# Factorization kernel, prologue and epilogue: linear-layer sums in another pool, one set of x sums on GpSimd, the last squares added on VectorE

## The chip, the cores and the metric

The kernel runs on one core of a Trainium2 chip. The metric is device time in microseconds (us), the median of several runs. The kernel before takes 1424.27 us (three runs, 1423.39 to 1424.46). All times inside the kernel are from one profiled execution of 1423.96 us, whose span of recorded work is 1422.2 us; a time such as "at 44.5" counts from the start of that span.

## What is computed

```python
def _L0_rec_ref(x, weight, lin_w, lin_b):      # x 1024x512, weight 64x512x512, float32
    out_lin = x @ lin_w.T + lin_b
    xv = jnp.einsum('bf,efm->bem', x, weight)
    zp = jnp.einsum('bf,efm->bem', jnp.square(x), jnp.square(weight))
    interaction = 0.5 * jnp.sum(jnp.square(xv) - zp, axis=1)
    return out_lin + interaction
```

The second product is linear in the squared weights, so the squares are summed over the 64 embeddings first and multiplied once, at the end. What remains is 64 products of a 1024x512 by a 512x512 matrix, each squared and summed.

## The kernel before

**Tiling.** Two embeddings are treated together (32 pairs, index `q`). Each pair is a 2x2 block problem that is solved with seven products in place of eight (Strassen's scheme in Winograd's form), and each of the seven is split once more in the same way. There are thus 7 outer products per pair, called "1" to "7" and run in the order 1, 2, 6, 5, 7, 3, 4, and 7 inner products in each. A product needs sums of blocks of x as the stationary operand (`xs`, for every outer and inner index, made once), sums of blocks of the weights as the moving operand (`to` for the outer sums, `ti` for the inner ones, made for each pair), and sums of results (`z`).

**Engines.** TensorE multiplies in float32; an inner product is two matmuls of 256 columns, each recorded as two. GpSimd makes `to` (line 321) and `ti` (lines 332, 339, 340) and issues the DMAs that add the squares to `acc[0]`, `acc[1]` (line 455) and the squared weights to `w2_sum` (line 475). VectorE makes the x sums (`outer_x`, lines 143 to 150; `inner_x`, 157 to 160; `a21_sums`, 224 to 227) before the loop, and adds TensorE's results from PSUM in it (lines 405, 407, 421). ScalarE copies PSUM banks and squares. SyncE loads weights and stores the result.

**Order.** Nothing is scheduled by a tool: `st.at(t, fn)` puts a piece of work at a time of a written-out schedule, and the list sorted by `t` is the order in which every engine receives its instructions, which it works off strictly one after the other. One unit of `t` in the loop is one inner product on TensorE. Pair q begins at 49 q; times below zero are the prologue. A pool hands out its buffers in turn, and who asks for one that is still being read waits for the reader: `zpool` (tag "z") has 6, `tipool` (tag "ti") 3, `topool` 3.

**The prologue.** TensorE first runs matmuls on constants (`spin`, lines 179 and 181), then `x @ lin_w.T`: the first half of the rows in 16 plain matmuls (`lin`, line 195), the second half (`lin_p`, line 241) with seven inner products for each half of the contraction. `lin_p("5")`, `("6")` and so on multiply by sums of lin_w in the two buffers `LT`, made by GpSimd at t = -30, with x sums from `A21_SUMS` (first half) and from `inner_x("4")` (second half). The two `LT` buffers come from `tipool`, as do the first pair's `ti` for products 1, 2, 6, 5. VectorE makes the x sums for outer products 1, 2, the A21 sums, 4, 5, then (after a `lin_join`, line 261, that waits for TensorE) 6, again a `lin_join`, then 7 and 3; after them comes its first work of the loop, `join("y", "s5", 3)` of product 1 (line 421, t = 8.5), which TensorE's seventh inner product of product 1 (t = 12) waits for, since both use PSUM bank y.

**The epilogue.** After the last pair (g = 49 x 32 = 1568) the product of squared x and summed squared weights is made for two groups of rows, s = 0 and s = 1, seven inner products of 8 recorded matmuls each (line 589). VectorE halves `acc` and adds the bias (`last_t`, line 618, two instructions for each s and r), adds that to blocks of the output (`add_t`, line 648), and combines PSUM banks (`minus_half`, line 635). Eight stores follow (line 643). `acc[1]` is complete only when the squares of the last `c21` have been added to it, at t = g + 9.65, by a DMA that GpSimd issues (line 455).

Of the kernel before, what the change touches and what calls it, by code (L numbers as in the profile page):

```python
# [8 lines left out]
F32 = mybir.dt.float32  # L9
# [19 lines left out]
def kernel(  # L29
# [30 lines left out]
    nc = tc.nc  # L60
    _, _, _, Q = x.shape
    E, F, M = weight.shape
    P = 128
    NK = F // P
    HM = M // 2
    BK = 2 * HM
# [4 lines left out]
    tipool = ctx.enter_context(tc.tile_pool(name="tipool", bufs=3))  # L71
    w2pool = ctx.enter_context(tc.tile_pool(name="w2pool", bufs=2))
    spool = ctx.enter_context(tc.tile_pool(name="spool", bufs=3))
    zpool = ctx.enter_context(tc.tile_pool(name="zpool", bufs=6))
# [8 lines left out]
    acc = [  # L83
        const.tile([P, 4, BK], F32, tag=f"acc{r}", name=f"acc{r}") for r in range(2)
    ]

    def xsl(i, o):
        return xs[:, SLOT[i], SLOT[o], :]

    st = Stream()  # L90
# [31 lines left out]
    def quarter(r, kk, n):  # L122

        w = slice(0, 3) if n is None else n
        for i, rk in BLOCK.items():
            if rk == (r, kk):
                return a21[i] if n == 3 else xs[:, SLOT[i], w, :]
        return A21[:, w, :]

    def outer_x(i):  # L130
        if i in BLOCK:
            return []

        def put(n):
            w = slice(0, 3) if n is None else n

            def of(o):
                return a21[o] if n == 3 else xs[:, SLOT[o], w, :]

            def src(r, kk):  # L140
                return quarter(r, kk, n)

            if i == "5":
                nc.vector.tensor_add(of(i), src(1, 0), src(1, 1))
            elif i == "6":
                nc.vector.tensor_sub(of(i), of("5"), src(0, 0))
            elif i == "7":
                nc.vector.tensor_sub(of(i), src(0, 0), src(1, 0))  # L148
            else:
                nc.vector.tensor_sub(of(i), src(0, 1), of("6"))  # L150

        return [lambda: put(None), lambda: put(3)]

    def inner_x(i):
        add, sub = nc.vector.tensor_add, nc.vector.tensor_sub
        return [
            lambda: add(xsl(i, "5"), a21[i], xsl(i, "4")),  # L157
            lambda: sub(xsl(i, "6"), xsl(i, "5"), xsl(i, "1")),
            lambda: sub(xsl(i, "7"), xsl(i, "1"), a21[i]),  # L159
            lambda: sub(xsl(i, "3"), xsl(i, "2"), xsl(i, "6")),  # L160
        ]
# [3 lines left out]


    A21_SUMS = zpool.tile([P, 4, Q], F32, tag="z", name="A21_sums")
    LT = [tipool.tile([P, 4, HM], F32, tag="ti", name=f"lt{kk}") for kk in range(2)]
    LIN = {}

    def spin():

        one = nc.const_aps.tensor(1.0, [P, BK], mybir.dt.bfloat16)
        zero = nc.const_aps.tensor(0.0, [P, BK], F32)
        for n in range(3):
            ps = psum.tile([P, BK], F32, tag="y", name=f"y_spin{n}", bufs=3)
            nc.tensor.matmul(ps, one[:, 0:P], one, start=True, stop=True)
        for _ in range(2):  # L180
            nc.tensor.matmul(ps, zero[:, 0:P], zero, start=True, stop=True)

    def lin(kk):

        order = [(s, j, l) for s in range(2) for j in range(2) for l in range(2)]
        if kk == 0:
            order.sort(key=lambda o: o[2])
        for s, j, l in order:
            n = 2 * s + j
            if kk == 0 and l == 0:  # L190
                tag = "xxvv"[n]
                LIN[n] = psum.tile(
                    [P, M], F32, tag=tag, name=f"lin{n}", bufs=2 if tag == "x" else 3
                )
            nc.tensor.matmul(  # L195
                LIN[n],
                quarter(0, kk, (0, 1, 3, 2)[2 * s + l])[:, ts(j, P)],
                lw_sb[:, 2 * kk + l, :],
                start=(kk == 0 and l == 0),
                stop=(kk == 1 and l == 1),  # L200
            )
# [10 lines left out]
    def lin_x(kk, o):  # L212
        if kk == 1:
            return xsl("4", o)
        return A21[:, SLOT[o]] if o in "124" else A21_SUMS[:, "5673".index(o)]
# [14 lines left out]
    def lin_p(o, bank, first):  # L230
        def fn():
# [7 lines left out]
            for kk in range(2):  # L239
                for j in range(2):  # L240
                    nc.tensor.matmul(  # L241
                        LIN[bank][:, ts(j, HM)],
                        lin_x(kk, o)[:, ts(j, P)],
                        operand_b(lw_sb[:, ts(kk, 2)], LT[kk], o),
                        start=(first and kk == 0 and j == 0),
# [13 lines left out]
    def lin_join(bank, s, blk):  # L259
# [5 lines left out]
        return fn  # L265

    st.at(-40, spin)
    for kk in range(2):
        st.at(-30 + 8 * kk, lambda kk=kk: lin(kk))
        st.at(-30 + kk, lambda kk=kk: sums_t(LT[kk], lw_sb[:, ts(kk, 2)]))  # L270
    for n in range(4):
# [70 lines left out]
    def inner_t(q, i):  # L342
        TI[q, i] = tipool.tile([P, 4, HM], F32, tag="ti", name=f"ti{q}_{i}")
        sums_t(TI[q, i], outer_b(q, i))

    def operand_b(b, t, o):
        return {
            "1": lambda: b[:, 0, 0:HM],
            "2": lambda: b[:, 1, 0:HM],
            "3": lambda: b[:, 1, HM:M],  # L350
            "5": lambda: t[:, 0, :],
            "7": lambda: t[:, 1, :],
            "6": lambda: t[:, 2, :],
            "4": lambda: t[:, 3, :],
        }[o]()
# [14 lines left out]
    Z = {}  # L370
# [74 lines left out]
    def squares(t, q, name, r, wait=5):  # L445
        def sq():
            z = Z[q, name]
            for h in range(2):
                o = z[:, ts(h, 2)]
                nc.scalar.activation(o, o, AF.Square)  # L450

        st.at(t, sq)
        st.at(
            t + wait,
            lambda: nc.gpsimd.dma_start(acc[r], Z[q, name], accum_op=ALU.add),  # L455
        )
# [32 lines left out]
    for q in range(NQ):  # L489
        g0 = 49 * q  # L490
        st.at(-100 if q == 0 else g0 - 48.8, lambda q=q: load_w(q))
        for n, i in enumerate(ORDER):
            t0 = g0 + 7 * n
            lead = t0 - 7.5
            if i == "6":
                st.at(lead - 8, lambda q=q: outer_t(q, "5"))
                st.at(lead - 4, lambda q=q: outer_t(q, "6"))
            if i == "7":
                st.at(lead - 4, lambda q=q: outer_t(q, "7"))
            if i == "4":  # L500
                st.at(lead - 1, lambda q=q: outer_t(q, "4"))
            st.at(lead, lambda q=q, i=i: inner_t(q, i))
            block_product(t0, q, i, SUMS[i])
            if i == "2":
                squares(t0 + 14.6, q, "c11", 0)
            if i == "7":
                squares(t0 + 14.6, q, "z5", 1)
            if i == "3":
                squares(t0 + 14.6, q, "c12", 0, 5 if q < NQ - 1 else 4)
            if i == "4":  # L510
                if q < NQ - 1:
                    squares(t0 + 14.6, q, "c21", 1)
                else:
                    squares(t0 + 12.65, q, "c21", 1, 1)
        for v in range(2):
            w_squares(g0 + 14.6 + 14 * v, q, v)


    for sums, t in (
        (inner_x("1"), -29),  # L520
        (inner_x("2"), -22),
        (a21_sums(), -20),
        (inner_x("4"), -18),
        *((outer_x(m) + inner_x(m), t) for m, t in zip("5673", (-16, -5, -3, -1))),
    ):
        for n, fn in enumerate(sums):
            st.at(t + 0.1 * n, fn)

    g = 49 * NQ
    h = g - 49
# [76 lines left out]
    def blk(n, s, b):  # L610
        return L[n, s][:, b // 2, b % 2]
# [4 lines left out]
    def last_t(s, r):  # L616
        for u in range(2):
            nc.vector.scalar_tensor_tensor(
                L["t", s][:, r, u].rearrange("p (j c) -> p j c", j=2),
                acc[r][:, 2 * s + u].rearrange("p (j c) -> p j c", j=2),  # L620
                0.5,
                bias[:, ts(u, HM)].unsqueeze(1).broadcast_to([P, 2, HM]),
                ALU.mult,
                ALU.add,
            )
# [15 lines left out]
    def store(s, b):  # L641
        r, u = b // 2, b % 2
        nc.sync.dma_start(
            out_dst[r, s, :, u], blk("o", s, b).rearrange("p (j c) -> p j c", j=2)
        )

    def add_t(s, b):
        nc.vector.tensor_add(blk("o", s, b), blk("o", s, b), blk("t", s, b))
# [8 lines left out]
    for s, ks in ((0, (0, 3.2, 5.2, 6, 7, 8, 9)), (1, (10, 12, 14, 16, 18, 20, 22))):  # L657
# [19 lines left out]
        else:  # L677
            st.at(k2 + 0.5, minus_half("x", s, 0, "t"))
            st.at(k4 + 0.5, minus_half("y", s, 2, "t"))
            for b, k in ((0, k2), (3, k7), (1, k3), (2, k4)):  # L680
                st.at(k + 0.6, lambda b=b: store(1, b))
    for r, t in ((0, 11), (1, 13)):
        st.at(g + t, lambda r=r: last_t(0, r))
        st.at(g + t + 0.1, lambda r=r: last_t(1, r))
        for u in range(2):
            st.at(g + t + 0.2, lambda b=2 * r + u: add_t(0, b))
            st.at(g + t + 0.2, lambda b=2 * r + u: store(0, b))
    for b in (3, 1):
        st.at(g + 15, lambda b=b: add_t(1, b))

    with tc.manual_schedule():
        st.run()
# [30 lines left out]
```

## Time and profile before

| | busy in the profile (span 1422.2 us) | share |
|---|---|---|
| TensorE matmul | 1411.8 us | 99% |
| GpSimd | 1174.4 us | 83% |
| VectorE | 922.2 us | 65% |
| ScalarE | 616.7 us | 43% |

[...]the 99% says who sets the time and not how much is left. The first 50 us and the last 20 us are where the change lies; there the order in time (start, duration, engine, line, operation, operands, count, and in brackets how long the engine had been idle and for whom) says more than the sums. The list of waits names who waited for whom, the total, how often, and the longest. The table by stretches gives the TensorE clock that was granted as a share of the full one.

### The profile page before, as it was taken

What the parts mean: (1) busy time and instruction counts of PE and PEld (TensorE: products, weight loads), DVE (VectorE), ACT (ScalarE), POOL (GpSimd) and SP (SyncE); (2) the same over time, 40 slices, a digit from 0 to 9 for tenths busy, and PEclk for the clock granted to TensorE, in tenths of its full rate; (3) what the DMA queues carried; (4) which work ended last, traced back from release to release, by engine and by line L of the source; (5) the groups of instructions that cost most, each with busy time, mean ns of one, the idle gap of its engine ahead of it and who ended that gap; (6) DMA issues with size and microseconds to landing.
All of it is one profiled execution on the core that took longest, in us unless ns stands there. A gap on an engine that the chain in (4) does not pass through costs nothing.

```text
span 1422.2 us, 18124 instructions
## 1 busy us (share of the span) xinstructions
PE 1411.8 (99%) x6479; PEld 1232.8 (87%) x6479; DVE 922.2 (65%) x1342; ACT 616.7 (43%) x822; POOL 1174.4 (83%) x1041
## 2 busy tenths in 40 slices
PE   9899999999999999999999999999999999999998
PEld 6788888888888888888888888888888888888887
DVE  6756667656667666666665666665666765666665
ACT  2354444454443444444444444445444345444352
POOL 4689888888888888888888888888988888888884
PEclk9999999999999999999999999999999999999999
DMA  5298888899889889889889888889888989998886
GB/s 207 50 212 202 200 197 194 193 204 207 199 197 202 185 194 215 200 200 201 187 189 218 200 200 202 183 198 213 200 200 196 198 189 202 207 203 197 203 175 148
DMA packets 41290, 276.16 MB, mean 194 GB/s; under 512 B 4465, under 2 KB 7025, under 8 KB 8561
## 3 DMA queue, kind: packets, MB, share of 16 engines
q0 software_dynamic: 27504, 200.29, 69.3%
q1 hardware_dynamic: 12976, 72.62, 17.2%
q10 hardware_dynamic: 720, 2.10, 0.4%
q8 instruction: 52, 0.85, 0.2%
q14 instruction: 38, 0.30, 0.1%
HBM read 72.61 MB, written 2.10 MB: 53 GB/s over the span
## 4 chain that ended last, share of the span: by engine, by line
PE 95%; DVE 1%; DMA 1%; POOL 1%; issue 0%; ACT 0%; POOLq 0%; SPq 0%; DVEq 0%
PE y L361 40%; PE x L361 27%; PE v L361 27%; PE lin L195 1%; DMA acc<-z_c 1%; DMA xs<-x 1%; PE y_lin L241 0%; PE x_lin L241 0%; POOL tw L579 0%; DVE a_sb L148 0%; POOL sx L564 0%; POOL z_z L415 0%; DVE xs L159 0%; POOL sx L562 0%; DVE xs L157 0%
## 5 line engine op out<-in xcount | busy, mean ns | idle before, releaser
L361 PE MATMUL y<-ti,xs 128*128 128x256 f32 x2688 | 654.7, 379 | 4.7 <-DVE z_z L421 4.7
L361 PEld LDWEIGHTS y<-ti,xs 128*128 128x128 f32 x2688 | 511.2, 190 | 74.9 <-DVE z_z L421 5.1
L426 ACT COPY y<-x 128x512 f32<-128x512 f32 x224 | 127.7, 570 | 620.8 <-PE x L361 620.8
L361 PE MATMUL x<-to,xs 128*128 128x256 f32 x1024 | 253.1, 380 | 0.0
L361 PE MATMUL v<-ti,xs 128*128 128x256 f32 x896 | 229.9, 379 | 0.0
L361 PEld LDWEIGHTS x<-to,xs 128*128 128x128 f32 x1024 | 195.1, 191 | 26.7
L332 POOL TENSOR_TENSOR ti<-to 128x512 f32<-128x512 f32 x128 | 180.9, 1413 | 33.8 <-PE y L361 30.5
L321 POOL TENSOR_TENSOR to<-w,to 128x1024 f32<-128x1024 f32 x64 | 159.5, 2491 | 45.6 <-PE v L361 45.6
L361 PE MATMUL x<-w,xs 128*128 128x256 f32 x768 | 192.8, 380 | 0.0
L450 ACT ACTIVATE z_c<-z_c 128x1024 f32<-128x1024 f32 x192 | 192.6, 1053 | 0.0
L361 PEld LDWEIGHTS v<-ti,xs 128*128 128x128 f32 x896 | 170.2, 190 | 23.1
L421 DVE TENSOR_TENSOR z_z<-y,s 128x512 f32<-128x512 f32 x128 | 88.0, 687 | 125.6 <-PE y L361 125.6
L361 PEld LDWEIGHTS x<-w,xs 128*128 128x128 f32 x768 | 146.5, 191 | 20.1
L332 POOL TENSOR_TENSOR ti<-w 128x512 f32<-128x512 f32 x96 | 131.0, 1365 | 32.8 <-PE y L361 19.8
L361 PE MATMUL v<-to,xs 128*128 128x256 f32 x512 | 131.4, 379 | 0.0
L455 POOL DMA_DIRECT2D acc<-z_c x96 | 84.1, 876 | 57.1 <-ACT z_c L450 48.4
L405 DVE TENSOR_TENSOR s<-y,z_z 128x512 f32<-128x512 f32 x160 | 110.3, 689 | 28.8 <-PE y L361 22.6
L467 ACT ACTIVATE w<-w 128x1024 f32<-128x1024 f32 x126 | 126.3, 1053 | 0.0
L421 DVE TENSOR_TENSOR z_c<-y,s 128x512 f32<-128x512 f32 x96 | 66.4, 692 | 90.3 <-PE y L361 90.3
L405 DVE TENSOR_TENSOR s<-v,z_z 128x512 f32<-128x512 f32 x160 | 110.1, 688 | 18.4 <-PE v L361 11.4
L421 DVE TENSOR_TENSOR z_z<-v,s 128x512 f32<-128x512 f32 x128 | 87.7, 685 | 38.2 <-PE v L361 38.2
L361 PEld LDWEIGHTS v<-to,xs 128*128 128x128 f32 x512 | 97.3, 190 | 13.2
(112 smaller groups left out, 1617.0 us busy)
## 6 DMA issues: line engine op xcount, KB each, us to landing
acc<-z_c POOLq DMA_DIRECT2D x96, 1024.0 KB, 7.6
w_sum<-w POOLq DMA_DIRECT2D x63, 1024.0 KB, 7.9
w<-weight SPq DMA_DIRECT2D x62, 1024.0 KB, 6.0
acc<-z_z POOLq DMA_DIRECT2D x32, 1024.0 KB, 7.8
xq<-x SPq DMA_DIRECT2D x2, 1024.0 KB, 5.5
out<-o_last SPq DMA_DIRECT2D x8, 256.0 KB, 2.3
w<-weight ACTq DMA_DIRECT2D x2, 512.0 KB, 8.8
w<-weight SPq DMA_DIRECT2D x2, 512.0 KB, 7.8
```

The source lines that it names most:

```text
L195: nc.tensor.matmul(LIN[n], quarter(0, kk, (0, 1, 3, 2)[2 * s + l])[:, ts(j, P)], lw_sb[:, 2 * kk + l, :], start=(kk == 0 and l == 0), stop ...
L321: nc.gpsimd.tensor_sub(t, a, b)
L332: nc.gpsimd.tensor_sub(t[:, 0:2, :], b[:, :, HM:M], b.rearrange("p l m -> p (l m)")[:, 0:M].rearrange("p (u c) -> p u c", u=2),)
L361: nc.tensor.matmul(ps[:, ts(j, HM)], xsl(i, o)[:, ts(j, P)], rhs, start=(start and j == 0), stop=True, skip_group_check=True,)
L405: nc.vector.tensor_add(o, d[bank], Z[q, addend][:, blk])
L421: nc.vector.tensor_add(Z[q, name][:, blk], d[bank], d[s])
L426: st.at(t0 + 0.5, lambda: nc.scalar.copy(d["y"], d["x"]))
L450: nc.scalar.activation(o, o, AF.Square)
L455: lambda: nc.gpsimd.dma_start(acc[r], Z[q, name], accum_op=ALU.add),
L467: nc.scalar.activation(w2[:, ts(h, 2)], W[q, v][:, ts(h, 2)], AF.Square)
```

## The change

It has five parts. The sums of lin_w move from two buffers of `tipool` to one of `zpool`, which is to leave all three `ti` buffers to the loop's first operands. The x sums of outer product 3 (six instructions: 768 columns, 256 columns, and four of 256) move from VectorE to GpSimd, and from t = -1 to t = 14 and after, since they are first read at t = 35. The second constant matmul group of `spin` loses half of one matmul. The squares of the last `c21` are added to `acc[1]` by two VectorE instructions of 1024 columns at t = g + 8.65 in place of the DMA. VectorE's last work is put in another order, so that what row group 1 needs comes before what only row group 0's second half needs.

```diff
-    def outer_x(i):
+    def outer_x(i, eng=nc.vector):
...
-    def inner_x(i):
-        add, sub = nc.vector.tensor_add, nc.vector.tensor_sub
+    def inner_x(i, eng=nc.vector):
+        add, sub = eng.tensor_add, eng.tensor_sub
...
-    LT = [tipool.tile([P, 4, HM], F32, tag="ti", name=f"lt{kk}") for kk in range(2)]
+    lt_sb = zpool.tile([P, 2, 4, HM], F32, tag="z", name="lt_sb")
+    LT = [lt_sb[:, kk] for kk in range(2)]
...
-        for _ in range(2):
-            nc.tensor.matmul(ps, zero[:, 0:P], zero, start=True, stop=True)
+        for n in (HM, BK):
+            nc.tensor.matmul(
+                ps[:, 0:n], zero[:, 0:P], zero[:, 0:n], start=True, stop=True
+            )
...
+        def add(h):
+            z = Z[q, name][:, ts(h, 2)]
+            nc.vector.tensor_add(acc[r][:, ts(h, 2)], acc[r][:, ts(h, 2)], z)
+
         st.at(t, sq)
+        if wait is None:
+            for h in range(2):
+                st.at(t + 3, lambda h=h: add(h))
+            return
...
-                    squares(t0 + 12.65, q, "c21", 1, 1)
+                    squares(t0 + 12.65, q, "c21", 1, None)
...
-        *((outer_x(m) + inner_x(m), t) for m, t in zip("5673", (-16, -5, -3, -1))),
+        *((outer_x(m) + inner_x(m), t) for m, t in zip("567", (-16, -5, -3))),
...
+    for n, fn in enumerate(outer_x("3", nc.gpsimd) + inner_x("3", nc.gpsimd)):
+        st.at(14 + n, fn)
...
-    for r, t in ((0, 11), (1, 13)):
-        st.at(g + t, lambda r=r: last_t(0, r))
-        st.at(g + t + 0.1, lambda r=r: last_t(1, r))
-        for u in range(2):
-            st.at(g + t + 0.2, lambda b=2 * r + u: add_t(0, b))
-            st.at(g + t + 0.2, lambda b=2 * r + u: store(0, b))
-    for b in (3, 1):
-        st.at(g + 15, lambda b=b: add_t(1, b))
+    for t, q, r in ((11, 0, 0), (11.1, 1, 0), (13, 1, 1), (18.7, 0, 1)):
+        st.at(g + t, lambda q=q, r=r: last_t(q, r))
+    for t, b in ((11.2, 0), (11.2, 1), (18.8, 2), (18.8, 3)):
+        st.at(g + t, lambda b=b: add_t(0, b))
+        st.at(g + t, lambda b=b: store(0, b))
+    for t, b in ((13.1, 3), (14.6, 1)):
+        st.at(g + t, lambda b=b: add_t(1, b))
```

More of the change, by code (lines that the diff above doesn't have):

```diff
@@ L143, in put @@
             if i == "5":
-                nc.vector.tensor_add(of(i), src(1, 0), src(1, 1))
+                eng.tensor_add(of(i), src(1, 0), src(1, 1))
             elif i == "6":
-                nc.vector.tensor_sub(of(i), of("5"), src(0, 0))
+                eng.tensor_sub(of(i), of("5"), src(0, 0))
             elif i == "7":
-                nc.vector.tensor_sub(of(i), src(0, 0), src(1, 0))
+                eng.tensor_sub(of(i), src(0, 0), src(1, 0))
             else:
-                nc.vector.tensor_sub(of(i), src(0, 1), of("6"))
+                eng.tensor_sub(of(i), src(0, 1), of("6"))
         return [lambda: put(None), lambda: put(3)]
-    def inner_x(i):
-        add, sub = nc.vector.tensor_add, nc.vector.tensor_sub
+    def inner_x(i, eng=nc.vector):
+        add, sub = eng.tensor_add, eng.tensor_sub
         return [
```

## The prediction, made before the changed kernel ran

> **What bounds the kernel now.** I read the page's shares first (TensorE matmul 99%), then the list of waits for what TensorE still waits on, then the first 50 us and last 20 us in order of time, then the granted clock by stretches. The list of waits has these lines on the change:
>
> ```profile
> POOL ti L332 <- PE y_lin L241: 13.0, 1, 13.0
> PE y L361 <- DVE z_z L421: 4.7, 1, 4.7
> DVE t_last L618 <- DMA acc<-z_c: 2.3, 1, 2.3
> PE y_last L589 <- DVE o_last L635: 0.7, 1, 0.7
> ```
>
> The columns are total us, times, longest. TensorE has two stalls of weight, each once. The first, in order of time:
>
> ```profile
> 43.78 0.68 DVE L421 TENSOR_TENSOR z_z<-y,s 128x512 f32<-128x512 f32 x1
> 44.52 2.07 PE L361 MATMUL y<-ti,xs 128*128 128x256 f32 x4 [4.73 <-DVE z_z L421]
> 46.39 1.91 PE L361 MATMUL x<-w,xs 128*128 128x256 f32 x4
> 48.09 1.78 PE L361 MATMUL x<-to,xs 128*128 128x256 f32 x4
> 49.72 1.03 PE L361 MATMUL y<-ti,xs 128*128 128x256 f32 x4
> ```
>
> The inner product before it started at 38.76 and one takes 0.863 us (start to start, 37.90 to 38.76), so undisturbed the fourth row would start at 38.76 + 4 x 0.863 = 42.2, not 49.72. The gap costs 7.5 us, of which only 4.9 are the wait: the next three products start 1.87, 1.70 and 1.63 us apart. The clock (eighth column) says why:
>
> ```profile
> 42.00:43.00 1.00, 0.00 (x0) 0.00 (x0) 0.93 (x3) 0.00 (x0) 0.00 (x0) 0.90 0.00 0
> 43.00:44.00 1.00, 0.00 (x0) 0.00 (x0) 1.00 (x4) 0.00 (x0) 0.00 (x0) 0.50 0.00 0
> 49.00:50.00 1.00, 1.00 (x5) 0.85 (x4) 0.03 (x1) 0.08 (x1) 1.00 (x2) 0.69 0.00 0
> ```
>
> It halved at 42.8 (0.90) and came back at 49.6 (0.69). VectorE was late because GpSimd held it up. Here is the pattern:
>
> ```profile
> 14.00 0.78 POOL L339 TENSOR_TENSOR ti<-w,ti 128x256 f32<-128x256 f32 x1
> 14.23 0.83 DVE L158 TENSOR_TENSOR xs<-xs 128x256 f32<-128x256 f32 x1
> 15.61 2.53 POOL L321 TENSOR_TENSOR to<-w,w 128x1024 f32<-128x1024 f32 x1
> 15.85 2.56 DVE L160 TENSOR_TENSOR xs<-xs 128x256 f32<-128x256 f32 x1
> 20.25 0.42 DVE L158 TENSOR_TENSOR xs<-xs 128x256 f32<-128x256 f32 x1
> ```
>
> Alone an x sum takes 0.42; beside GpSimd it ends 0.27 us after the GpSimd instruction does (14.78 to 15.06, 18.14 to 18.41), so the two alternate, one each. VectorE's instructions that read PSUM keep 0.68 beside GpSimd. From 18.1 to 31.1 GpSimd waits for an `LT` buffer; its 9 us of work for products 2 and 6 then falls on VectorE's last sums (31 to 40.5).
>
> [...]
>
> **LT in the big pool.** `ti` 2 no longer waits 13 us. `ti` 2, `to` 6 and `ti` 6 (1.45 + 0.78 + 0.79, 2.53, 1.4 + 0.8 + 0.8) run from 18.2 to about 27.2. That relieves 31 to 40, but VectorE's sums between 18.3 and 21.3, until now free, alternate with them. Ends worked out with the 0.27 us: A21 "5" after 18.22 + 1.45, at 19.95; "6" at 20.8; "7" at 21.65; "3" behind `to` 6 (21.4 to 24.0) at 24.3; x4 "5" behind `ti` 6's first (24.05 to 25.5) at 25.75; x4 "6" at 26.6; x4 "7" at 27.45. TensorE needs x4 "5" for the second half of `lin_p("5")`, which before loaded weights at 22.02:
>
> ```profile
> 22.02 0.84 PEld L241 LDWEIGHTS v_lin<-lt,xs 128*128 128x128 f32 x4
> ```
>
> So a new stall of about 25.8 - 22.05 = 3.75 us takes the place of the old wait. "6" is needed 1.7 us after that (27.5) and "7" later, so one stall. Behind it everything shifts by 3.75. GpSimd is then idle until about 44 (it waits for `ti` 1), so VectorE's 6, 7 and two joins run at their free pace: y join at 32.2, 6 done 35.5, v join 36.2, 7 done 39.0; TensorE gives `join("y")` its bank at 36.17 + 3.75 + 1 = 40.9. With product 3's sums gone (2.8 us, 41.00 to 43.78) the old stall is gone whole: -7.5.
>
> Does the new stall halve the clock? TensorE idles about 3.6 us[...]. [...]four runs within 1.1 us suggest that it halved in all of them[...]. I take two in three. [...]
>
> **x sums of product 3 on GpSimd.** No GpSimd instruction of 768 columns is in the trace: between 1.26 (512) and 2.37 (1024), taken 1.8. With five of 256 at 0.8 pitch that is 5.8 us. They queue behind `ti` 5 (done 47.1) and around `to` 7; behind them stands `ti` 7, first part done 56.4. TensorE wants it at product index 27, 31.73 + 3.75 + 27 x 0.863 = 58.8. Margin 2.4 us; `to` 7 has 4, `ti` 3 over 4, and the x sums themselves (55.1) 4 before 59.2. GpSimd's 17% idle absorbs the rest: 0. The later release of `raw_sb` holds `z5` until 49.7, wanted at 56.5: 0.
>
> **Shorter spin.** 0.86 us less of cold matmul, but `lin` then waits for x until 9.27 as now (it already idles 0.33 there): 0.
>
> **The end.** Undisturbed the last product starts at 1413.78 + 1.73 = 1415.5, not 1416.35: 0.85 lost. New VectorE order: two adds of 1024 columns, from pitches 0.34, 0.60 and 0.87 for 256, 512 and 768 about 1.14 each, 1404.2 to 1406.5; four halvings and two adds at 0.6 to 1410.1; two and two to 1412.5; x block; y block 1414.0 to 1414.7, in time for 1415.5. Then two halvings and two adds to 1417.05, v block to 1417.65, last block 1417.65 to 1418.3 where TensorE would allow 1417.5. Against 1419.07: -0.8. The two stores of row group 0 now stand just before the last two; three stores 0.6 apart landed after 2.2, 2.4, 2.5 us, the lone last one after 2.2, so a fourth lands after 2.65: +0.4. Net -0.4.
>
> **Sum, likeliest case.** -7.5 + 3.75 + 1.9 - 0.4 = -2.2, from 1424.0 (the profiled run) to 1424.27 (median): 1421.8 to 1422.0. I take 1421.8.
>
> **Rivals.**
> A, the stall moves but the clock stays full: -4.15, 1420.0. [...] Against: the old stall seems to have halved it every time. 25%.
> B, the forecast, 1420.9 to 1422.9: 45%.
> C, VectorE slips one sum ahead (then 2.2 us of stall and no halving, 1418.4) or GpSimd's early work doesn't hold it up at all (-7.9, 1416.3). Against: at 14.00, 14.86 and 15.61 GpSimd went first each time. 12%.
> D, no gain or slower. The sums on GpSimd take 50% longer (5.8 to 8.7 us), which overruns the margin of `ti` 7 and is passed on to TensorE nearly whole (+2.9), the halving costs its upper bound (3.4 in place of 1.9: +1.5), the stores queue one more time over (+1): 1421.8 + 5.4 = 1427.2; with one of the three alone 1422.8 to 1424.7. Against: margins of 2.4 to 4 us and 17% idle. 18%, of which under half is over 1427.1.
>
> **Numbers.** 0.2% is 2.85 us: 1421.4 and 1427.1. Faster: A 25, C 12, a third of B 15, together 52%; slower 8% (of D); same 40%. Range: 1418.4 to 1424.2 leaves out half of C and most of D.
>
> **What would show it.** Right: TensorE waiting some 3.7 us for an x sum in `lin_p` near 22, GpSimd busy without a break from 12.5 to 27, no wait for VectorE near 40, clock halved at some time between 25 and 33, last product without a wait. Wrong: VectorE's sums of 0.42 us between 18 and 22 beside a busy GpSimd, a wait of TensorE for `ti` 7 near 59, or the last store over 3 us after its block.

## The result and the profile after

The changed kernel takes 1420.59 us (eight runs, 1416.80 to 1422.02) against 1423.94 us before (eight runs, 1423.32 to 1424.46): ratio 0.9973, 95% interval 0.9962 to 0.9984. It is faster by 3.4 us, and its runs are spread over 5 us where those of before lay within 1.1. The profiled run took 1421.11 us, its span 1419.3 us.

The list of waits of the changed kernel (who waited for whom: us in total, times, longest), the lines in which TensorE waits for another engine after the first 10 us. `PEld` is its weight load:

```profile
PEld v_lin L244 <- POOL ti L335: 3.6, 1, 3.6
PE v_lin L244 <- DVE xs L157: 3.2, 1, 3.2
```

Both waits for VectorE that the list of before had, in the loop and at the last product, are gone. One new one, in `lin_p("5")`, stands in their place. (The first line names GpSimd, but its instruction had ended at 24.98, and this product doesn't read `ti`: of the two operands, `lt_sb` was complete at 12.3, and VectorE's sum came at 25.27.) In order of time (start, duration, engine, line, what; in brackets the idle time before):

```profile
17.93 1.44 POOL L335 TENSOR_TENSOR ti<-w 128x512 f32<-128x512 f32 x1
18.17 1.48 DVE L227 TENSOR_TENSOR A_sums<-raw_sb 128x256 f32<-128x256 f32 x1
...
21.07 2.52 POOL L324 TENSOR_TENSOR to<-w,to 128x1024 f32<-128x1024 f32 x1
21.31 2.56 DVE L230 TENSOR_TENSOR A_sums<-raw_sb,A_sums 128x256 f32<-128x256 f32 x1
23.66 1.32 POOL L335 TENSOR_TENSOR ti<-to 128x512 f32<-128x512 f32 x1
23.79 1.48 DVE L157 TENSOR_TENSOR xs<-raw_sb,xs 128x256 f32<-128x256 f32 x1
25.41 1.10 PE L244 MATMUL v_lin<-lt_sb,xs 128*128 128x256 f32 x4 [3.19 <-DVE xs L157]
...
42.25 0.69 DVE L424 TENSOR_TENSOR z_z<-y,s 128x512 f32<-128x512 f32 x1 [1.88 <-PE y L364]
```

GpSimd no longer waits for a buffer and works without a break from 18 to 26.7. VectorE's sums, 0.42 us each in the kernel before at this place, take 0.8 to 2.6 us, one behind each GpSimd instruction; the x4 sum that TensorE waits for ends at 25.3. In the last row the join of product 1 has waited for TensorE (1.88 us), where before TensorE waited for it. The clock of the changed kernel, in the table by stretches (eighth column, as before):

```profile
26.00:27.00 1.00, 1.00 (x6) 0.90 (x5) 1.00 (x3) 0.45 (x1) 0.72 (x1) 0.91 0.00 0
27.00:28.00 1.00, 1.00 (x3) 0.76 (x3) 1.00 (x3) 0.15 (x1) 0.00 (x0) 0.50 0.00 0
30.00:31.00 1.00, 1.00 (x5) 0.83 (x5) 0.13 (x1) 0.21 (x1) 0.00 (x0) 0.88 0.00 0
```

It halved here too, after the new wait, from 26.8 to 30.2: 3.4 us, of which half is lost.

**Where the time went.** Three stretches account for the two profiled runs: from VectorE's first x sum (the moment x has landed and TensorE can go on with `lin`) to the first product of the loop; from there to the 13th product; from the loop's last matmul to the end.

| us | before | after |
|---|---|---|
| x has landed | 9.23 | 9.06 |
| to the loop's first product | 22.50 | 27.61 |
| its first 12 products | 17.98 | 10.49 |
| from the loop's last matmul to the end | 25.9 | 25.6 |

So -7.5 in the loop, +5.1 ahead of it (3.4 of stall and 1.7 of halved clock), -0.3 at the end, -0.2 from the landing of x: -2.9, the difference of the spans.

### The profile page after: what moved, and what is told of

Its sections match the earlier page's. It is cut to its first block, busy times and chain, and to the rows that moved or that the text cites. A ratio compares the mean times of both kernels' runs of the same rounds, so it can differ in the third digit from the quotient of the medians.

```text
span 1419.3 us, 18121 instructions
## 1 busy us (share of the span) xinstructions
PE 1410.8 (99%) x6479; PEld 1232.5 (87%) x6479; DVE 923.2 (65%) x1338; ACT 616.9 (43%) x822; POOL 1179.0 (83%) x1046
## 4 chain that ended last, share of the span: by engine, by line
PE 98%; DVE 1%; DMA 1%; issue 0%; SPq 0%; DVEq 0%
PE y L364 41%; PE x L364 27%; PE v L364 27%; PE y_last L603 1%; DMA xs<-x 1%; PE x_last L603 0%; PE y_lin L244 0%; PE v_last L603 0%; DVE xs L160 0%; DVE xs L157 0%; PE v_lin L244 0%; DVE A_sums L230 0%; DVE xs L158 0%; PE x_lin L244 0%; DVE xs L159 0%; DVE A_sums L227 0%
```

## The experiments

All times are medians beside the kernel before on the same chip, of which there were three (the kernel before took 1423.43, 1423.58 and 1423.82 us on them). Ratios carry 95% intervals. Most runs left no trace, but each has its mean granted clock on record. A stretch of 3.4 us at half clock lowers it by 0.0012, so a run at 1.000 had none. A run at 0.999 may have had one or not, since the clock can also fall once the matmuls are over: in the profiled run of before it was 0.70 from 1421.5 to the end at 1422.2, the last matmul having ended at 1418.3, and the profiled runs of `a_delay` and `a_reorder` have 0.999 without a halved stretch in their first 50 us. No profiled run without such a stretch is below 0.999, so a run at 0.998 is taken to have had at least one.

### The two parts of the prologue, one undone at a time

`a_lt_back` is the changed kernel with the old buffers for the sums of lin_w:

```diff
-    lt_sb = zpool.tile([P, 2, 4, HM], F32, tag="z", name="lt_sb")
-    LT = [lt_sb[:, kk] for kk in range(2)]
+    LT = [tipool.tile([P, 4, HM], F32, tag="ti", name=f"lt{kk}") for kk in range(2)]
```

> The changed kernel with the sums of lin_w back in two tipool buffers, nothing else undone. Theory (moving these sums trades the old stall near 40 for a new one near 22): GpSimd waits again until about 31, no stall near 22; VectorE is free at 41.0 instead of 43.8, so TensorE waits about 2 us near 40[...]: 1423.94 - 7.5 + 2.0 - 0.4 = 1418.0 us, faster than the changed kernel and with less spread than its 5 us. Rival (the gain comes from moving these sums): about 1423.5 us.

Measured 1419.75 us, 0.997 (0.9961 to 0.998), from 1417.88 to 1420.75. The stall near 22 is gone and one of 2 us stands near 40, as expected. In order of time, and below it the clock by stretches:

```profile
41.15 0.68 DVE L423 TENSOR_TENSOR z_z<-y,s 128x512 f32<-128x512 f32 x1
41.88 1.97 PE L363 MATMUL y<-ti,xs 128*128 128x256 f32 x4 [1.94 <-DVE z_z L423]
```

```profile
41.00:42.00 1.00, 0.12 (x1) 0.12 (x2) 0.90 (x3) 0.00 (x0) 0.00 (x0) 1.00 0.00 0
42.00:43.00 1.00, 1.00 (x3) 0.82 (x4) 1.00 (x2) 0.00 (x0) 0.00 (x0) 0.51 0.00 0
```

But the clock halved after it, at 42.0 and for 3.4 us, which the expected 1418.0 has no term for. That costs 1.7 us, as much as the median missed the expectation of 1418.0 by; the three runs with a mean clock of 1.000 took 1417.88, 1417.90 and 1418.94. In this run, then, a wait of 1.94 us went with a halving.

`a_x3_back` is the changed kernel with the sums of product 3 on VectorE again:

```diff
-        *((outer_x(m) + inner_x(m), t) for m, t in zip("567", (-16, -5, -3))),
+        *((outer_x(m) + inner_x(m), t) for m, t in zip("5673", (-16, -5, -3, -1))),
...
-    for n, fn in enumerate(outer_x("3", nc.gpsimd) + inner_x("3", nc.gpsimd)):
-        st.at(14 + n, fn)
```

> The changed kernel with the x sums of product 3 back on VectorE at t = -1. Theory: once GpSimd is idle from 27 to 45, VectorE makes these sums unhindered in 2.8 us before TensorE needs the join, so nothing is lost: 1420.6 us, with the same stall near 22. Rival (these sums leaving VectorE is what removes the old stall): 2.8 us of wait near 42, 1423.4 us.

Measured 1418.56 us, 0.9966 (0.9954 to 0.9979), from 1417.10 to 1421.46: nothing is lost, the rival's 1423.4 is out. That it came out below 1420.6 was not expected, but it lies inside the spread of the changed kernel. Its profiled run (1417.10) shows what a quick run is like:

```profile
8.97 0.42 DVE L157 TENSOR_TENSOR xs<-raw_sb,xs 128x256 f32<-128x256 f32 x1 [8.97 <-DMA xs<-x]
9.43 0.42 DVE L158 TENSOR_TENSOR xs<-xs 128x256 f32<-128x256 f32 x1
9.77 0.42 DVE L159 TENSOR_TENSOR xs<-xs,raw_sb 128x256 f32<-128x256 f32 x1
9.98 1.34 POOL L335 TENSOR_TENSOR lt_sb<-lw_sb 128x512 f32<-128x512 f32 x1 [1.15 <-DMA lw_sb<-lin_wT]
```

The second half of lin_w landed a microsecond after x, so VectorE had begun three sums before GpSimd's second set of lin_w sums began. In the changed kernel's profiled run it had begun one (9.06; GpSimd began at 9.23). Two sums more of a lead are two GpSimd instructions less to wait behind: TensorE's waits ahead of the loop came to 1.2 us in place of 5.1 with the halving.

### Each part alone

`b_lt` is the kernel before with the zpool buffer alone (the first diff reversed); `b_x3` the kernel before with product 3's sums on GpSimd alone.

> The kernel before with nothing changed but the sums of lin_w in a zpool buffer. Theory (this part alone trades the old stall for the one near 22; the x sums of product 3 can stay on VectorE): as the changed kernel but for the end, 1418.5 to 1421 us with its spread of several us. Rival (both parts are needed): 1422 us or more, with a wait of TensorE for VectorE near 42.

> The kernel before with nothing changed but the x sums of product 3 on GpSimd. Theory: the wait near 40 falls from 4.9 to about 2.2 us, the clock still halves after it in most runs[...]: 1423.8 - 2.8 - 0.9 = 1420.1 us, from 1418 to 1421. Rival (the sums on GpSimd hold up ti 7): 1422 or more.

Measured 1418.83 us, 0.9966 (0.9954 to 0.9978), and 1418.84 us, 0.9969 (0.9957 to 0.9981). Either alone gains what both together gain, or more: they are two ways to remove one stall, of which `b_x3` keeps 2 us and `b_lt` nothing, with the new stall in its place. `b_lt` lies within its expectation. `b_x3` is 1.3 us below its own, which had the clock halve in most runs: it did not in the profiled run, and four of six runs have a mean clock of 1.000. Waits of TensorE in `b_lt`, then in `b_x3`:

```profile
PE v_lin L242 <- DVE xs L157: 2.9, 1, 2.9
```

```profile
PE y L361 <- DVE z_z L421: 1.9, 1, 1.9
```

### What the new stall is made of

`a_reorder` is the changed kernel with VectorE's sums in the order in which TensorE wants them:

```diff
-        (inner_x("2"), -22),
+        (inner_x("2"), -17),
...
-        *((outer_x(m) + inner_x(m), t) for m, t in zip("567", (-16, -5, -3))),
+        *((outer_x(m) + inner_x(m), t) for m, t in zip("567", (-5.49, -5, -3))),
```

> The changed kernel with VectorE's first sums in another order: those of x4 right after the A21 sums, those of x2 and x5 (needed only from product 2 and 5 on) after them, x5 behind the first join. The work and GpSimd's queue are the same, so VectorE and GpSimd still alternate. Theory (the stall near 22 is VectorE's x4 sums queued behind 12 others, each held up by one GpSimd instruction): x4 '5' is ready near 21.4, TensorE waits at most 0.5 us near 22 and nowhere else, no halving: 1423.5 - 7.5 + 0.5 - 0.4 = 1416.1 us, with a spread near 1 us. Rival (TensorE would wait for something else there, or the joins behind the moved sums come late): 1418.5 or more.

Measured 1416.02 us, 0.9948 (0.9936 to 0.9959), four of five runs from 1415.68 to 1416.24 and one at 1418.38. It beats both kernels. The alternation is as before, and hurts nobody (in order of time):

```profile
19.54 0.94 DVE L157 TENSOR_TENSOR xs<-raw_sb,xs 128x256 f32<-128x256 f32 x1
...
21.28 2.56 DVE L159 TENSOR_TENSOR xs<-xs,raw_sb 128x256 f32<-128x256 f32 x1
...
22.09 1.03 PE L244 MATMUL v_lin<-lt_sb,xs 128*128 128x256 f32 x4
...
38.00 0.68 DVE L424 TENSOR_TENSOR z_z<-y,s 128x512 f32<-128x512 f32 x1
```

The x4 "5" sum is ready at 20.5, TensorE takes it at 22.09 without a wait, and the first product of the loop starts 22.50 us after x has landed, as in the kernel before. The last row is the join that had started at 43.78 there.

`a_reorder_x3` is this kernel with product 3's sums back on VectorE (the second diff above).

> The kernel with VectorE's first sums reordered, and the x sums of product 3 back on VectorE at t = -1. Theory (with the sums of lin_w in zpool, moving product 3's sums to GpSimd gains nothing): VectorE has them done before it is wanted, or is at most 1 us late: 1416.0 to 1417 us. Rival (moving them is needed, as the kernel before suggests where they were the last 2.8 us): 1418.5 or more.

Measured 1418.34 us, 0.9965 (0.9953 to 0.9978): the rival is nearer. Without the stall near 22, TensorE is early, and VectorE, with 2.8 us more to do, is the later one:

```profile
40.00 0.42 DVE L160 TENSOR_TENSOR xs<-xs 128x256 f32<-128x256 f32 x1
40.34 0.68 DVE L424 TENSOR_TENSOR z_z<-y,s 128x512 f32<-128x512 f32 x1
41.08 1.42 PE L364 MATMUL y<-ti,xs 128*128 128x256 f32 x4 [2.20 <-DVE z_z L424]
```

So the move of these sums is worth nothing in the changed kernel and about 2.3 us in the reordered one (the two were run on different chips, with 0.24 us between their kernels before). The shorter path of TensorE is half of the reason. Counted from the landing of x, the join of product 1 began at 30.7 in the profiled run of `a_x3_back` and TensorE wanted its bank at 31.6; here it began at 32.0 and was wanted at 30.4. That VectorE is 1.3 us later comes with the new order: it waited 3.7 us for a part of x, until 13.6, where in `a_x3_back` it waited 0.4. This is one profiled run of each.

`a_delay` gives GpSimd a useless instruction more, ahead of its second set of lin_w sums:

```diff
     st.at(-40, spin)
+    st.at(-29.5, lambda: nc.gpsimd.memset(acc[0], 0.0))
```

> The changed kernel with one useless GpSimd instruction more: a memset of 2048 columns of acc[0] (overwritten later) between the two halves of the sums of lin_w, so that all of GpSimd's early work starts 1 to 2 us later. Theory (the long stall near 22, and with it the spread, comes from GpSimd's second half of these sums starting within 0.2 us of VectorE's first x sum, so that the two alternate from the start; where it started 1 us later the stall was 0.9): VectorE gets 3 or 4 sums ahead, the stall falls below 1 us, no halving: about 1416.5 us with a spread near 1 us, 4 us faster for 2 us of added work. Rival ([...]GpSimd's work is what TensorE waits for): 1420.6 us or slower, spread as before.

Measured 1417.42 us, 0.9957 (0.9944 to 0.9969), all five runs from 1417.33 to 1417.75. Work added to a busy engine makes the kernel 3 to 4 us faster than the changed kernel and takes its spread away. In order of time:

```profile
8.88 1.81 POOL L271 MEMSET acc<- 128x2048 f32 x1
9.26 0.42 DVE L158 TENSOR_TENSOR xs<-xs 128x256 f32<-128x256 f32 x1
9.60 0.42 DVE L159 TENSOR_TENSOR xs<-xs,raw_sb 128x256 f32<-128x256 f32 x1
9.94 0.42 DVE L160 TENSOR_TENSOR xs<-xs 128x256 f32<-128x256 f32 x1
10.65 1.26 POOL L336 TENSOR_TENSOR lt_sb<-lw_sb 128x512 f32<-128x512 f32 x1
```

This GpSimd instruction, which reads no tensor, did not hold up the three of VectorE's sums that ran whole beside it: at 9.26, 9.60 and 9.94 they took 0.42 us each, where the sums beside GpSimd's own sums took 0.8 to 2.6. What is left against 1416 is a wait of 1.1 us for the first `lin_join`, which stands behind the x5 sums in VectorE's queue; the reordering had moved that too.

### The clock

`a_fill` puts twelve matmuls on constants, whose result is not used, ahead of the waiting product:

```diff
+    SPIN = []
...
+            SPIN.append(ps)
...
             for kk in range(2):
+                if o == "5" and kk == 1:
+                    one = nc.const_aps.tensor(1.0, [P, BK], mybir.dt.bfloat16)
+                    for _ in range(12):
+                        nc.tensor.matmul(
+                            SPIN[2], one[:, 0:P], one, start=True, stop=True
+                        )
```

> The changed kernel with twelve extra bf16 matmuls on constants put in TensorE's queue just ahead of the inner product that waits near 22 (about 2.6 us of work inside the wait; their result is not used). Theory (the changed kernel's time is the stall plus, in most runs, a halved clock after it): the wait ends at the same moment, the clock stays full, 1417 to 1419.4 us, little spread. Rival (the spread has another cause): 1420.6 us and the spread stays.

Measured 1418.59 us, 0.997 (0.9959 to 0.9981). Four of seven runs lie between 1418.29 and 1418.59, the others go up to 1421.05. The profiled one is the slowest. In order of time, and below it the clock by stretches:

```profile
9.84 8.80 PE L200 MATMUL lin<-lw_sb,xs 128*128 128x512 f32 x16 [1.96 <-DMA xs<-x]
...
26.05 0.83 DVE L158 TENSOR_TENSOR xs<-xs 128x256 f32<-128x256 f32 x1
...
27.12 1.02 PE L252 MATMUL v_lin<-lt_sb,xs 128*128 128x256 f32 x4
```

```profile
10.00:11.00 1.00, 1.00 (x3) 0.52 (x3) 0.97 (x2) 0.00 (x0) 1.00 (x1) 0.91 1.03 419
28.00:29.00 1.00, 1.00 (x6) 0.90 (x5) 1.00 (x3) 0.60 (x1) 0.00 (x0) 1.00 0.00 0
```

Nothing halved after the filled wait, but the clock had halved at 10.8, after a wait of 2.0 us for x in `lin`. That made `lin` late, so the filling outlasted the wait: the x4 "5" sum was done at 26.0, and the product behind the twelve matmuls began at 27.12. So the median came out where the theory had it (1417 to 1419.4), and the spread of 2.8 us did not go. In this run the delay comes from the first 10 us; for the others that is not shown.

`a_spin_back` is the changed kernel with the old, longer constant matmuls; `a_again` the changed kernel as it is, to have its spread beside these.

> The changed kernel with the old constant matmuls (0.86 us longer). Theory: lin waits for x until about 9.3 in both, and later for VectorE: 1420.6 us, no difference. Rival (the shorter constant work leaves a gap of up to 2.5 us ahead of 9.5 that halves the clock by itself, as seen in the run with matmuls filled in): about 1 us faster and less spread.

> The changed kernel as it is, to have its spread beside the others on the same chip. All theories: 1420.6 us, from 1416.8 to 1422.

Measured 1420.02 us (0.9973, 0.9963 to 0.9983; 1417.47 to 1421.45) and 1421.20 us (0.998, 0.9972 to 0.9988; 1417.03 to 1423.23). The difference is inside the spread; the runs don't tell whether the shorter spin does anything. (The gap of 2.5 us in the expectation counts from the start of one matmul to the start of the next; the wait in it was 2.0.) It can matter: in the profiled run of `b_x3` (old spin) `lin` was slower at its beginning, its first four matmul records taking 2.40 us from 5.42 to the next ones, where those of `b_lt` (old spin too) took 1.77 from the same moment, as if the clock had come to full only near 6.7 (an estimate from these two, with half the full speed until then); x landed at 8.5, and `lin` reached it at 9.5, a microsecond late. The profiled run of `a_again`, 1423.23 us, is the bad end of the spread: x landed at 10.06, GpSimd began at 10.21, and the clock was halved for 6.8 us, 25.3 to 32.1. Against the 1421.11 us of the first profiled run that is 1.0 for the landing and 1.15 for the clock.

### The end

`b_tail` is the kernel before with only the end changed (`squares`, `add`, and the two loops over `last_t`, `add_t`, `store`, as in the diff of the change).

> The kernel before with only the end changed: last squares added by VectorE, new order of its last work. Theory: TensorE's 0.85 us wait for VectorE goes, 0.4 comes back as a later landing of the last store: 1423.94 - 0.4 = 1423.5 us. Rival (stores queue more): no change or up to 0.5 slower.

Measured 1423.45 us, ratio 1.0 (0.9992 to 1.0008). The interval of 1.1 us to either side cannot show 0.4. The trace does: from the loop's last matmul to the end 25.6 us, as in the changed kernel, against 25.9 before. VectorE's last two instructions and the clearing of the stores in the changed kernel, in order of time and by stretches (last two columns: share of the DMA engines, GB/s):

```profile
1414.44 0.68 DVE L649 SCALAR_TENSOR_TENSOR o_last<-v_last,o_last 128x512 f32<-128x512 f32 x1
1415.04 0.68 DVE L649 SCALAR_TENSOR_TENSOR o_last<-y_last,t_last 128x512 f32<-128x512 f32 x1
```

```profile
1415.00:1416.00 1.00, 0.00 (x0) 0.00 (x0) 0.72 (x2) 0.00 (x0) 0.00 (x0) 1.00 1.02 332
1416.00:1417.00 1.00, 0.00 (x0) 0.00 (x0) 0.00 (x0) 0.00 (x0) 0.00 (x0) 1.00 1.04 349
1417.00:1418.00 1.00, 0.00 (x0) 0.00 (x0) 0.00 (x0) 0.00 (x0) 0.00 (x0) 1.00 0.96 319
```

The DMA engines are busy nearly without a break for three microseconds (a share of 0.96 to 1.04). The last four stores, issued 0.6 us apart, landed 2.2, 2.3, 2.5 and 2.7 us after their issue, where the lone one of before took 2.2.

### All profiled runs in one table

"Lead" is from VectorE's first x sum to GpSimd's second set of lin_w sums; "to loop" from the same moment to the loop's first product (22.50 undisturbed); "12 products" as above (10.48 undisturbed). The clock is that of the first 50 us, once it has come to full (in the changed kernel's profiled run the weight loads of `lin` took 0.33 us at 5.43 and 0.19 from 6.75 on).

| kernel | lead | to loop | 12 products | clock halved | run, us |
|---|---|---|---|---|---|
| before | 0.25 | 22.50 | 17.98 | 42.8 to 49.6 | 1423.96 |
| `b_tail` | 0.20 | 22.50 | 17.97 | 43.0 to 49.8 | 1423.90 |
| after | 0.17 | 27.61 | 10.49 | 26.8 to 30.2 | 1421.11 |
| `a_again` | 0.15 | 28.74 | 10.48 | 25.3 to 32.1 | 1423.23 |
| `b_lt` | 0.19 | 27.72 | 10.48 | 26.0 to 29.4 | 1420.93 |
| `a_x3_back` | 1.01 | 23.71 | 10.48 | no | 1417.10 |
| `a_spin_back` | 1.49 | 24.20 | 10.49 | no | 1417.47 |
| `a_delay` | 1.95 | 24.26 | 10.49 | no | 1417.39 |
| `a_lt_back` | 0.19 | 22.49 | 14.38 | 42.0 to 45.4 | 1420.20 |
| `b_x3` | 0.19 | 23.44 | 12.69 | no | 1418.87 |
| `a_reorder_x3` | 1.72 | 22.50 | 14.64 | 41.8 to 45.2 | 1419.38 |
| `a_reorder` | 0.24 | 22.50 | 10.48 | no | 1416.02 |
| `a_fill` | 0.18 | 26.82 | 10.48 | 10.8 to 14.2 | 1421.05 |

Among the kernels that have the zpool buffer and the old order of sums, a lead of 0.2 goes with 5 us and more ahead of the loop, one of 1 us or more with less than 2 (`a_fill`, whose wait is filled, stands apart). `a_delay` sets the lead on purpose and has all its runs at the quick end.

## Why the prediction was right

The median, 1420.59, lies between the forecast's case B (1420.9 to 1422.9) and rival A (1420.0, the clock stays full), and is nearer to A than to the 1421.8 itself. It is the traces that speak for B: all terms are in the profiled run, the clock among them. They add up to -2.9 us there where the prediction had -2.2: 0.4 for the shorter new stall, 0.2 for the clock, 0.2 for an earlier landing of x, and 0.1 lost at the end.

**The old stall** was put at 7.5 us, 4.9 of wait and 2.6 of halved clock, and said to go whole: 17.98 became 10.49. That this needs only one of the two parts was not in the prediction; `b_lt` shows it for the buffer; the x sums alone leave 2 us (`b_x3`, `a_lt_back`).

**The new stall in `lin_p`** was named at its place and with its cause, 3.75 us long. Measured 3.4 between what would have been the start and 25.41: the x4 sum ended at 25.3 and not 25.75, because x had landed 0.2 earlier and GpSimd's work up to there was 0.3 us shorter in sum (its instruction at 23.66 took 1.32, taken 1.45). `a_reorder` and `a_delay` show the cause: change only VectorE's order, or only GpSimd's start, and the stall goes.

**The clock** was given two chances in three to halve, and the sum takes 1.9 us for it. The 1.9 was the author's estimate; what the trace of before shows is one stretch of 6.8 us at half clock, half of which is the 3.4 of rival D. It cost 1.7 in the first profiled run and 2.85 in the second (`a_again`). Of the eight runs of the changed kernel, five have a mean clock of 0.998, and the profiled one, at 0.999, halved too. Only the two quickest, 1416.80 and 1417.93, have 1.000.

**Rival C was taken as a rare slip of VectorE; it is more common than that.** How long after x the second half of lin_w lands decides VectorE's lead, and it differs from run to run: 0.15 to 1.72 us in the table, `a_delay` apart. The prediction's argument against C, that GpSimd went first at 14.00, 14.86 and 15.61, was an observation of one run. The runs of 1416.80 and 1417.93 beat the profiled one by 4.3 and 3.2 us, more than the 1.7 of the halved clock. A longer lead would account for the rest, and so in part would an earlier landing of x (8.3 to 10.1 in the profiled runs); no trace of these runs was kept, so which it was is not shown.

**GpSimd's margins** held: the 768 columns took 1.82 us (taken 1.8), `ti` 7's first part was done at 57.4 (56.4 in the prediction, which did not shift its times by the halved clock), and 28 products later (from the 13th to the 41st) TensorE stood as far on as in the kernel before, 24.17 us in both. **The end** came out at -0.3 for -0.4. **The spin** is not settled by the totals, as said above.

## What to carry to other kernels

Two edits that each remove the same stall don't add up; before combining them, ask which wait ends last once the first has done its work. GpSimd set free early is not free: here, beside a busy GpSimd, VectorE's sums of x ended one behind each of GpSimd's, and took up to 2.56 us in place of 0.42. So what is queued on VectorE should stand in the order in which TensorE wants it (`a_reorder`, 1416.02 us for 1420.59). Where a kernel's spread grows with a change, look for two transfers whose order of landing decides who goes first.

## What was not expected of the hardware

Waits of the same length ended differently. In the profiled run of `a_lt_back` one of 1.94 us went with a halving, at 42.0 and for 3.4 us. In that of `b_x3` one of 1.9 us, at the same product of the loop, did not: from 40 to 44, over the wait and two microseconds behind it, the granted clock was 1.00 throughout. `lin`'s wait for x is much the same case: 1.96 us with a halving in `a_fill`, 1.81 in `a_again` without one behind it (its weight loads still took 0.19 us at 12.74).

How long the clock stays low does not follow from the wait either. One of 3.19 us in `lin_p` went with 3.4 us at half clock in the changed kernel and, just as long, with 6.8 in `a_again`, where the clock fell 1.1 us before the wait was over. In the table it is 3.4 or 6.8 each time. What else decides whether and for how long the clock halves, these runs don't show.

A useless memset of 1.8 us on GpSimd made the kernel over 3 us faster (`a_delay`, 1417.42 for 1420.59).
